# Streaming a weight block's columns in shorter runs: five half groups of an embedding interaction kernel

## The chip, the cores and the metric

The kernel runs on one core of a Trainium2 chip. The core has a matrix engine (TensorE, PE in the profile, whose weight loads have a row of their own, PEld), a vector engine (DVE), a scalar engine (ACT), a general engine (GpSimd, POOL) and a queue engine that starts transfers (SyncE, SP). Two memories on the core matter here: SBUF, which holds the operands, and PSUM, into which PE writes and adds up its results. The metric is the device time of one execution in microseconds; lower is better.

## The reference

For a batch `x` of 1024 rows with 512 features, and a weight tensor `W` of 64 embeddings by 512 features by 512 outputs, the reference computes

```
out_lin     = x @ lin_w.T + lin_b                              # 1024 x 512
xv          = einsum('bf,efm->bem', x, weight)                 # 1024 x 64 x 512
zp          = einsum('bf,efm->bem', x**2, weight**2)
interaction = 0.5 * sum over e of (xv**2 - zp)                 # 1024 x 512
out         = out_lin + interaction
```

Nearly all of the work is `xv`: for each of the 512 outputs ("features" in the title of the change: columns of the result), 64 embeddings of a 512 long dot product, for 1024 rows. It is squared and summed over the 64 embeddings. The sum over `e` doesn't depend on the order of the embeddings, and the order in which the columns are worked through changes no value, as long as each product lands at its own place.

## The kernel before

**Layout.** Before the launch, W is laid out so that one block of it, 128 partitions by 2 by 512, holds in each row of 512 the columns of 8 outputs (`MI = 8`) with 64 embeddings each (`E = 64`): column number = 64 * output + embedding. So the 64 embeddings of one output lie next to each other, 256 bytes of float32. Two such half blocks per group and 16 groups (`NG`) make 32 half groups (`NH`), numbered `h` from 0 to 31.

**Products.** In each half group the matrix product is cut by a Strassen-like scheme into seven block products, numbered 1 to 7 and worked in the order of `ORDER = (1, 6, 2, 3, 7, 5, 4)`; product 5 in that row is the one of the next half group. The seven sums of the blocks of x (`X1` to `X7`) are made once at the start, and the sums of the blocks of W for each half group by transfers that add and by DVE.

**Three pieces.** PE takes each operand in a reduced float32 form, so W's block is split by ACT, POOL and DVE into a high, a low and a combined piece (`pH`, `pL`, `pK`, made in `split`), and so is x (`X1H`, `X1L`, `X1K` and so on). A product is the sum of three: H by H and L by L (`front`), and later K by K (`back`), with a step of DVE or ACT that scales the bank in between. `mm` (L708 to L714) issues them. Each matmul keeps 128 by 128 of x as the stationary operand (the `lhsT`) and streams 512 columns of a piece of W past it, writing them into one PSUM bank (`buf[bank, j]`, 128 by 512 float32). In a half group these are 7 products by 2 halves by 2 banks by 3 pieces by 2 parts of the contraction = 168 matmuls.

**After a product.** DVE or ACT takes the banks: products 1 and 5 are kept in SBUF (`p1`, `p5`), others are added to those, and for products 2, 3, 7 and 4 `finish` squares the finished bank with ACT (L369, `sq<-bank`) and DVE sums the squares over the embeddings (L394, `acc<-sq`). These read the banks in storage order.

**Order.** The whole program is first collected in a `Plan`, which is given a cost for each operation (`PASS`, 0.2267 us for a matmul of this kind) and a fixed order for PE (`key`), and works out one fixed order of instructions for each engine. PE's matmuls of one product's `back` stand some steps after its `front` (`LAG`), between those of the next product.

**Ends.** At the start PE does the linear part in full float32 (L520, L531); at the end it does the product of the squares, `zp`, from sums already taken over the embeddings (L870).

Of the kernel before, what the change touches and what calls it, by code (L numbers as in the profile page):

```python
# [18 lines left out]
P = 128  # L19
# [16 lines left out]
PIECES = {"H": 3, "L": 3, "K": 3}  # L36
SQ, WSQ = 2, 1
PAIRS = {"p1": 2, "w": 2, "p5": 3}

NONE = ""  # L40

# [224 lines left out]
def kernel(  # L266
# [31 lines left out]
    MI = MG // 4  # L298
# [15 lines left out]
    buf = {}  # L314
# [14 lines left out]
    def ring(tag, n, shape, dtype=F32, pool=sb):  # L329
        return ring_of([make(f"{tag}_{i}", shape, dtype, pool) for i in range(n)])  # L330
# [7 lines left out]
    square, wsquare = ring("sq", SQ, block), ring("wsq", WSQ, block)  # L338
    kept = {n: ring(n, size, block) for n, size in PAIRS.items()}
    pairs = [f"{n}_{i}" for n, size in PAIRS.items() for i in range(size)]  # L340
    for n in pairs:
# [7 lines left out]
    def both_of(n):  # L349
        return (n, 0), (n, 1)  # L350
# [16 lines left out]
    def act(o, i, func, reads, writes, size=1024, scale=1.0, bias=0.0):  # L367
        def emit(_):
            nc.scalar.activation(o, i, func, bias=bias, scale=scale)  # L369

        plan.add({ACT: 0.06 + 0.89 * size / 1024}, emit, reads, writes)

    def stt(o, i, scalar, j, op, reads, writes, size=512, both=False):
        def emit(_):
            return nc.vector.scalar_tensor_tensor(o, i, scalar, j, ALU.mult, op)  # L375

        plan.add({DVE: 0.06 + 1.08 * size / 1024}, emit, reads, writes, both=both)

    def dve(o, a, b, sub, reads, writes, size=512, both=False):
        def emit(_):  # L380
            return (nc.vector.tensor_sub if sub else nc.vector.tensor_add)(o, a, b)  # L381

        plan.add({DVE: 0.06 + 1.08 * size / 1024}, emit, reads, writes, both=both)
# [73 lines left out]
    def a_parts(*names):  # L457
        return tuple((n, k) for n in names if n in quads for k in range(KH)) + tuple(
            n for n in names if n not in quads)
# [50 lines left out]
    def four():  # L510
        return [both_of(banks()) for _ in range(4)]
# [142 lines left out]
    def prepare(h, p):  # L654
        if p == 5:
            if h:
                load(h, "T", 0)
                load_more(h, "T", 1)
                load(h, "w11", 0)
                load(h, "w12", 1)  # L660
            else:
                sum_of("T", "w11", "w12")
            w_squares(h, "w12")
        if p == 1:
            if h:
                load(h, "w22", 3)
            else:
                for q in (0, 1, 3, 2):
                    load(h, QUAD[q], q)
            w_squares(h, "w11")  # L670
        if p == 6:
            if h:
                load_more(h, "T", 3)
                load(h, "w21", 2)
            else:
                sum_of("T", "T", "w22")
            w_squares(h, "w22")
        if p == 2:
            w_squares(h, "w21")
        if p == 7:  # L680
            load_more(h, "w12", 3)
        if p == 4:
            load_more(h, "T", 2)
        n = now[h, RHS[p]]
        return n if not h and p in PLAIN else split(n, SPLIT[p] if h else FIRST[p])
# [5 lines left out]
    def finish(h, p, half, bank):  # L691

        row, col = {2: (0, 0), 3: (0, 1), 4: (1, 0), 7: (1, 1)}[p]
        sq, a, names = square(), acc_name[h // NCB], both_of(bank)
        m, b = (2 * col + h % NCB) * MI, row * NJ + 2 * half
        if p == 7:
            n, p5 = value["w", h, half], value["p5", h, half]
            dve(buf[n], buf[bank], buf[p5], True, (p5, *names), (n, *names), 1024)
        act(buf[sq], buf[bank], AF.Square, names, (sq,), scale=S)
        reduce(buf[a][:, b:b + 2, m:m + MI], buf[sq], (sq,), ((a, b // 2, m),))  # L700

    def product(h, p):
        ops, plain = prepare(h, p), not h and p in PLAIN
        for half in range(2):
            bank = banks()
            o, names = buf[bank], both_of(bank)

            def mm(x, w, j, first, bank=bank, half=half):  # L708
                for k in range(KH):
                    made = nc.tensor.matmul(  # L710
                        buf[bank, j], buf[x][:, k, ts(2 * half + j, P)], buf[w][:, k, :],
                        start=first and k == 0, stop=k == KH - 1, skip_group_check=True,
                    )
                return made  # L714

            addend = {6: "p1", 2: "p1", 3: "w", 7: "w", 4: "w"}.get(p)
            addend = addend and value[addend, h, half]
            given = addend and (addend, *names)
            for j in range(2):
                at = slot[0]  # L720
                slot[0] += 1
                if plain:
                    x = OPERAND[p]
                    plan.add({PE: 2 * WHOLE}, lambda _, mm=mm, j=j: mm(x, ops, j, True),
                             (*a_parts(x), ops), ((bank, j),), key=at)
                    continue

                def front(_, mm=mm, j=j):
                    mm(f"X{p}H", ops[0], j, True)
                    return mm(f"X{p}L", ops[1], j, False)  # L730

                def back(_, mm=mm, j=j):
                    return mm(f"X{p}K", ops[2], j, False)

                plan.add({PE: 4 * PASS}, front, (f"X{p}H", f"X{p}L", *ops[:2]), ((bank, j),),
                         key=at)
                late.append((back, (f"X{p}K", ops[2], (bank, j)), (bank, j), slot[0] - j))
            if plain:
                if addend:
                    stt(o, o, U, buf[addend], ALU.add, given, names, 1024)  # L740
            else:
                if addend:
                    stt(o, o, 1 + U, buf[addend], ALU.add, given, names, 1024)
                elif SCALE[p] == ACT:
                    act(o, o, AF.Copy, names, names, scale=1 + U)
                else:
                    plan.add({DVE: 1.14}, lambda _, o=o: nc.vector.tensor_scalar(
                        o, o, 1 + U, None, ALU.mult), names, names)
                for back, reads, write, at in late:
                    plan.add({PE: 2 * PASS}, back, reads, (write,), key=at + LAG + 0.5 + 0.1 * write[1])  # L750
                late.clear()
            if p in (1, 5):
                n = value[f"p{p}", h, half] = kept[f"p{p}"]()
                act(buf[n], o, AF.Copy, names, (n,), scale=U if plain else 1.0)
            if p == 6:
                n, p5 = kept["w"](), value["p5", h, half]
                value["w", h, half] = n
                dve(buf[n], o, buf[p5], False, (p5, *names), (n,), 1024)
            if p in (2, 3, 7, 4):
                finish(h, p, half, bank)  # L760
# [24 lines left out]
    for h in range(NH):  # L785
        for p in ORDER:
            if p != 5:
                product(h, p)
            elif h + 1 < NH:
                product(h + 1, p)  # L790
            if not h and p == 1:
                product(h, 5)
            if not h:
                give_back(*(n for n in ("A11", "A12", "A22") if OPERAND[p] == n))
        if h % NCB == NCB - 1 and h + 1 < NH:
            turn(h // NCB)
# [5 lines left out]
    for r, pieces in enumerate((("X5H", "X5L", "X5K"), ("X1H", "X1L", "X1K"))):  # L802
# [7 lines left out]
        else:  # L810
            half = (("w2h", r),)
# [30 lines left out]
    for (r, c), n in zip(BLOCKS, ("p1", "p1", "p5", "p5")):  # L842
        n = o_name[r, c] = kept[n]()
# [41 lines left out]
    b = four()  # L885
    key = slot[0]
    for at, (r, c) in enumerate(BLOCKS):
        n = o_name[r, c]
# [63 lines left out]
```

## Time and profile before

| | |
|---|---|
| time, median of 2 runs | 1282.32 us (1282.12 and 1282.51) |
| profiled execution, first to last instruction (span) | 1280.3 us; its time with what lies around the span is not listed apart |
| PE, matmuls | 1274.3 us busy, 5524 instructions |
| PEld, weight loads | 1033.4 us busy, 5524 instructions |
| DVE | 1233.0 us busy |
| POOL | 1053.9 us busy |
| ACT | 967.0 us busy |
| granted PE clock | 1.000 |

How to read it: busy time is the time in which an engine has at least one instruction under way. [...] A full float32 matmul shows as two rows in the profile, so 38 of them make the profile's 5524 rows out of 5486 matmuls of the program.

### The profile page before, as it was taken

Reading aid. Unit: us, or ns where it says so; the run is one execution under the profiler, and the core shown is the slowest. Engines: PE = TensorE matmul, PEld = TensorE weight load, DVE = VectorE, ACT = ScalarE, POOL = GpSimd, SP = SyncE. Lnnn points to the kernel's source line nnn. Section 1 sums busy time; section 2 is a strip of 40 time slices with the busy share of each in tenths; the row PEclk is TensorE's granted clock in tenths of the full one; section 3 lists DMA queues with packets and bytes.
Section 4 is the critical chain, followed back from the end, with each engine's and each line's share of the span. In section 5 each row is a group of like instructions: output and inputs, shape, how many; then the busy total and the mean of one; then the engine's idle time right before and its main releaser. Section 6 shows DMA issues by size and latency. Waiting matters only on the chain.

```text
span 1280.3 us, 15588 instructions
## 1 busy us (share of the span) xinstructions
PE 1274.3 (100%) x5524; PEld 1033.4 (81%) x5524; DVE 1233.0 (96%) x1014; ACT 967.0 (76%) x1008; POOL 1053.9 (82%) x533
## 2 busy tenths in 40 slices
PE   9999999999999999999999999999999999999998
PEld 4788888888888888888888888888888888888886
DVE  6999999999999999999999999999999999999997
ACT  7677787777787777877677877777788777788891
POOL 2988898888898888898888898888888888889884
PEclk9999999999999999999999999999999999999999
DMA  7766654446664555755455664555665444664647
GB/s 229 176 173 146 148 129 109 105 119 140 148 142 109 95 122 133 153 130 135 92 115 130 148 153 102 115 115 117 152 146 130 102 106 119 148 152 117 138 99 184
DMA packets 67646, 170.36 MB, mean 133 GB/s; under 512 B 22896, under 2 KB 23920, under 8 KB 67568
## 3 DMA queue, kind: packets, MB, share of 16 engines
q0 software_dynamic: 20160, 71.84, 30.7%
q1 hardware_dynamic: 45584, 95.18, 25.6%
q10 hardware_dynamic: 1824, 2.36, 0.5%
q8 instruction: 43, 0.70, 0.2%
q14 instruction: 35, 0.29, 0.1%
HBM read 158.86 MB, written 6.29 MB: 129 GB/s over the span
## 4 chain that ended last, share of the span: by engine, by line
PE 97%; DVE 2%; ACT 1%; issue 0%; DVEq 0%; ACTq 0%
PE bank L710 93%; PE bank L870 2%; PE bank L531 1%; DVE bank L375 1%; PE bank L520 1%; DVE acc L394 1%; PE bank L548 0%; DVE w L381 0%; ACT sq L369 0%; DVE w_sum L394 0%; DVE X1K L375 0%; DVE p L375 0%; DVE X1L L375 0%; ACT pL L369 0%; ACT pH L369 0%
## 5 line engine op out<-in xcount | busy, mean ns | idle before, releaser
L387 POOL TENSOR_TENSOR pK<-pH,pL 128x1024 fp32r<-128x1024 f32 x224 | 591.1, 2639 | 180.2 <-PE bank L710 169.5
L369 ACT ACTIVATE sq<-bank 128x1024 f32<-128x1024 f32 x256 | 261.9, 1023 | 93.2 <-issue 46.8
L394 DVE TENSOR_REDUCE acc<-sq 128x16 f32<-128x1024 f32 x256 | 308.0, 1204 | 0.2 <-ACT sq L369 0.2
L387 POOL TENSOR_TENSOR pL<-T,pL 128x1024 fp32r<-128x1024 f32 x95 | 238.1, 2506 | 1.0 <-ACT pL L369 1.0
L375 DVE SCALAR_TENSOR_TENSOR bank<-bank,w 128x1024 f32<-128x1024 f32 x192 | 234.2, 1220 | 0.4
L381 DVE TENSOR_TENSOR w<-bank,p 128x1024 f32<-128x1024 f32 x128 | 155.6, 1216 | 25.1 <-PE bank L710 25.1
L387 POOL TENSOR_TENSOR pL<-w,pL 128x1024 fp32r<-128x1024 f32 x65 | 175.4, 2699 | 0.0
L369 ACT ACTIVATE p<-bank 128x1024 f32<-128x1024 f32 x128 | 131.0, 1023 | 56.0 <-PE bank L710 56.0
L375 DVE SCALAR_TENSOR_TENSOR pL<-pH,w 128x1024 fp32r<-128x1024 f32 x62 | 168.1, 2712 | 0.0
L369 ACT ACTIVATE pL<-T 128x1024 fp32r<-128x1024 f32 x95 | 100.0, 1053 | 73.4 <-issue 71.0
L394 DVE TENSOR_REDUCE w_sum<-wsq 128x16 f32<-128x1024 f32 x128 | 154.3, 1205 | 0.0
L375 DVE SCALAR_TENSOR_TENSOR bank<-bank,p 128x1024 f32<-128x1024 f32 x128 | 152.9, 1216 | 0.0
L369 ACT ACTIVATE pH<-w 128x1024 fp32r<-128x1024 f32 x128 | 135.2, 1056 | 11.6 <-PE bank L710 11.3
L369 ACT ACTIVATE wsq<-w 128x1024 f32<-128x1024 f32 x128 | 135.0, 1054 | 4.0 <-DVE w_sum L394 4.0
L369 ACT ACTIVATE pL<-w 128x1024 fp32r<-128x1024 f32 x66 | 70.0, 1061 | 43.4 <-PE bank L710 25.0
L369 ACT ACTIVATE pH<-T 128x1024 fp32r<-128x1024 f32 x96 | 101.2, 1054 | 0.0
L406 POOL DMA_DIRECT2D T<-weight x94 | 83.3, 981 | 9.1 <-POOL pL L387 9.0
L710 PE MATMUL bank<-pH,X4H 128*128 128x512 f32 x256 | 81.4, 399 | 0.1
L710 PE MATMUL bank<-pH,X5H 128*128 128x512 f32 x256 | 79.2, 391 | 0.0
L710 PE MATMUL bank<-pL,X4L 128*128 128x512 f32 x256 | 79.2, 390 | 0.0
L710 PE MATMUL bank<-pL,X5L 128*128 128x512 f32 x256 | 78.8, 389 | 0.0
L710 PE MATMUL bank<-pH,X6H 128*128 128x512 f32 x256 | 78.8, 389 | 0.0
(142 smaller groups left out, 2586.5 us busy)
## 6 DMA issues: line engine op xcount, KB each, us to landing
w<-weight SPq DMA_DIRECT2D x128, 512.0 KB, 7.5
T<-weight POOLq DMA_DIRECT2D x94, 512.0 KB, 7.4
w<-weight POOLq DMA_DIRECT2D x32, 512.0 KB, 10.2
T<-weight SPq DMA_DIRECT2D x31, 512.0 KB, 6.2
accd<-turned SPq DMA_DIRECT2D x64, 32.0 KB, 8.5
p<-lind SPq DMA_DIRECT2D x4, 512.0 KB, 3.6
w<-xT SPq DMA_DIRECT2D x6, 256.0 KB, 5.3
lind<-p SPq DMA_DIRECT2D x3, 512.0 KB, 3.6
```

Source lines behind the costliest of these rows:

```text
L369: nc.scalar.activation(o, i, func, bias=bias, scale=scale)
L375: return nc.vector.scalar_tensor_tensor(o, i, scalar, j, ALU.mult, op)
L381: return (nc.vector.tensor_sub if sub else nc.vector.tensor_add)(o, a, b)
L387: return (nc.gpsimd.tensor_sub if sub else nc.gpsimd.tensor_add)(o, a, b)
L394: lambda _: nc.vector.tensor_reduce(o, i.rearrange("p a (m e) -> p a m e", e=E), axis=AX.X, op=ALU.add),
L406: {POOL: 0.62}, lambda _: nc.gpsimd.dma_start(o, i, accum_op=ALU.add),
L520: return nc.tensor.matmul(buf[bank[u]], b[:, k, ts(u, P)], a[:, k, :], start=first and k == 0, stop=k == KH - 1, skip_group_check=True,)
L531: made = nc.tensor.matmul(buf[bank[u]], b[:, k, ts(u, P)], a[:, k, :], start=first and k == 0, stop=k == KH - 1, skip_group_check=True,)
L710: made = nc.tensor.matmul(buf[bank, j], buf[x][:, k, ts(2 * half + j, P)], buf[w][:, k, :], start=first and k == 0, stop=k == KH - 1, skip ...
L870: made = nc.tensor.matmul(buf[bank[u]], w[:, k, (2 * c + u) * P:(2 * c + u + 1) * P], x[:, k, :], start=z == 0 and i == which[0] and k == ...
```

## The change

A table `ORDERS` names five half groups and a number of parts for each: half group 4 with 2 parts, 7 with 4, 10 with 8, 13 with 16 and 16 with 32. In these, `in_order` gives the matmul another view of the same 512 columns, for the moving operand and for the PSUM bank alike: the 64 embeddings of each output are cut into that many parts, and the columns are streamed part by part, in each part output by output, in each output the part's embeddings. With 2 parts a run of neighbouring columns is 32 long (128 bytes), with 32 parts it is 2 long (8 bytes), and from run to run the address jumps by 256 bytes, or back to the next part. Each column still lands at its own place. The stationary operand, the pieces and what reads the banks afterwards stay as they are.

```diff
+ORDERS = {
+    4: 2, 7: 4, 10: 8, 13: 16, 16: 32,
+}
...
+            def in_order(a):
+                n = ORDERS.get(h)
+                return a if n is None else a.rearrange("p (m a b) -> p a m b", m=MI, a=n)
+
             def mm(x, w, j, first, bank=bank, half=half):
                 for k in range(KH):
                     made = nc.tensor.matmul(
-                        buf[bank, j], buf[x][:, k, ts(2 * half + j, P)], buf[w][:, k, :],
+                        in_order(buf[bank, j]), buf[x][:, k, ts(2 * half + j, P)],
+                        in_order(buf[w][:, k, :]),
                         start=first and k == 0, stop=k == KH - 1, skip_group_check=True,
                     )
```

On PE, at the place where half group 16 begins (its product 5, between the matmuls of half group 15's products 3, 7 and 4), the program has these rows before the change. A row names the line, the bank, the piece of W and the piece of x, the shape written, and how many equal ones follow each other.

```order
L710 MATMUL bank_117<-pK_101,X3K 128x512 x4
L710 MATMUL bank_116<-pH_97,X5H 128x512 x2
L710 MATMUL bank_116<-pL_100,X5L 128x512 x2
L710 MATMUL bank_116<-pH_97,X5H 128x512 x2
L710 MATMUL bank_116<-pL_100,X5L 128x512 x2
L710 MATMUL bank_114<-pK_102,X7K 128x512 x4
L710 MATMUL bank_117<-pH_97,X5H 128x512 x2
```

At the same place the changed program has these:

```order
L717 MATMUL bank_117<-pK_101,X3K 128x512 x4
L717 MATMUL bank_116<-pH_97,X5H 128x32x8x2 x2
L717 MATMUL bank_116<-pL_100,X5L 128x32x8x2 x2
L717 MATMUL bank_116<-pH_97,X5H 128x32x8x2 x2
L717 MATMUL bank_116<-pL_100,X5L 128x32x8x2 x2
L717 MATMUL bank_114<-pK_102,X7K 128x512 x4
L717 MATMUL bank_117<-pH_97,X5H 128x32x8x2 x2
```

Nothing has moved: the shape written has become 32 parts by 8 outputs by 2 embeddings in the rows of half group 16, and the line number is 717 for 710. On PE again, where half group 4 begins, the changed program has the rows below; before the change all of them read 128x512.

```order
L717 MATMUL bank_116<-pH_97,X5H 128x2x8x32 x2
L717 MATMUL bank_116<-pL_100,X5L 128x2x8x32 x2
L717 MATMUL bank_114<-pK_102,X7K 128x512 x4
L717 MATMUL bank_117<-pH_97,X5H 128x2x8x32 x2
L717 MATMUL bank_117<-pL_100,X5L 128x2x8x32 x2
L717 MATMUL bank_115<-pK_102,X7K 128x512 x4
```

Over the whole program the shape is another in 5 by 168 = 840 matmuls. No row stands at another place on PE, and on DVE, ACT, POOL and SP the rows are the same apart from the line numbers.

## The prediction, made before the changed kernel ran

> **What bounds the kernel now.** I read the shares of busy time first, then PE's waits, then the chain that ends last, and then PE's rows one by one. On the page of the kernel before:
>
> ```profile
> PE 1274.3 (100%) x5524; PEld 1033.4 (81%) x5524; DVE 1233.0 (96%) x1014; ACT 967.0 (76%) x1008; POOL 1053.9 (82%) x533
> ...
> PEclk9999999999999999999999999999999999999999
> ...
> PE 97%; DVE 2%; ACT 1%; issue 0%; DVEq 0%; ACTq 0%
> PE bank L710 93%; PE bank L870 2%; PE bank L531 1%; DVE bank L375 1%; PE bank L520 1%; DVE acc L394 1%; PE bank L548 0%; DVE w L381 0%; ACT sq L369 0%; DVE w_sum L394 0%; DVE X1K L375 0%; DVE p L375 0%; DVE X1L L375 0%; ACT pL L369 0%; ACT pH L369 0%
> ```
>
> PE is busy for the whole span and makes up 97% of the chain that ended last, 93% of it on the one line that the change edits. A busy PE alone says little, because its rows overlap. What counts is whether it ever waits. The view of PE's waits has two rows:
>
> ```profile
> PE bank L870 <- ACT sq L369: 1.0, 1, 1.0
> PE bank L548 <- PEq L941: 0.8, 1, 0.8
> ```
>
> Two waits in 1280 us, 1.8 us together, and both outside the main loop. DVE at 96% is close behind, but it never holds PE up. So the time is the number of matmuls by the distance from one to the next, and there is nowhere for a slower matmul to hide. The view of the waits of all engines shows that the others stand behind PE:
>
> ```profile
> POOL pK L387 <- PE bank L710: 169.5, 91, 3.0
> ACT p L369 <- PE bank L710: 56.0, 48, 1.7
> DVE w L381 <- PE bank L710: 25.1, 59, 0.6
> ```
>
> PE's distance is read from its rows in order of time (start, length of the merged row, what):
>
> ```profile
> 200.52 1.07 PE L710 MATMUL bank<-pK,X6K 128*128 128x512 f32 x4
> 201.43 0.62 PE L710 MATMUL bank<-pH,X2H 128*128 128x512 f32 x2
> ...
> 202.78 0.62 PE L710 MATMUL bank<-pL,X2L 128*128 128x512 f32 x2
> 203.24 1.07 PE L710 MATMUL bank<-pK,X6K 128*128 128x512 f32 x4
> ```
>
> From 200.52 to 203.24 us are 12 matmuls (4, then 8), 2.72 us, so **0.2267 us a matmul**, or 0.443 ns for each of its 512 columns. A half group of 168 takes 168 x 0.2267 = 38.1 us, and the five that change 190.4 us.
>
> **The change part by part.**
>
> *Nothing is removed, added or moved.* The five half groups have the same 840 matmuls, weight loads, banks, transfers and waits at the same places, so the term of the instruction count is zero, and no wait is added behind which anything could queue. Only the addresses differ that PE walks through in reading W's piece and in writing the bank. A pass could not get shorter by that: it streams the same 512 columns, and PE has no wait to lose but those 1.8 us. The lower bound is therefore nothing.
>
> *What a jump in the addresses costs PE* no row of this trace shows: every matmul of the loop reads and writes 128x512 in one run. I bound it from above by rows of slower walks over the same tiles. The first is PE's own, in the linear part, full float32, two rows to a matmul:
>
> ```profile
> 22.80 7.03 PE L531 MATMUL bank<-w,p 128*128 128x512 f32 x16
> 29.67 4.88 PE L710 MATMUL bank<-w,w 128*128 128x512 f32 x11
> ```
>
> 16 rows in 29.67 - 22.80 = 6.87 us are 0.4294 us for 512 columns, 0.203 us over 0.2267: PE at about half pace. The second is ACT, which reads two banks, 1024 columns, in 1.023 us:
>
> ```profile
> L369 ACT ACTIVATE sq<-bank 128x1024 f32<-128x1024 f32 x256 | 261.9, 1023 | 93.2 <-issue 46.8
> ```
>
> That is 1.0 ns a column, so 512 columns in 0.512 us, 0.285 over a matmul. By these, 840 matmuls would cost 840 x 0.203 = 170 us at PE's half pace and 840 x 0.285 = 239 us at ACT's, and nothing at full pace. The bounds are far apart, so the form of the cost decides. The five half groups cut the run by two each time: 32, 16, 8, 4 and 2 columns. If memory hands out values in portions, a run costs nothing while it fills whole portions and the pace halves at the first run that fills half of one. Where that step lies the trace doesn't say. The nearest supported price for a step is PE's own half pace, and the likeliest place is the shortest run, since it is hit in every case in which any is.
>
> **The sum I take:** half groups 4, 7, 10 and 13 at nothing, half group 16 at half pace. The price of half pace lies between 0.4294 - 0.2267 = 0.203 us (PE's float32 row) and 0.2267 us (a matmul twice as long): 168 x 0.203 = 34 us to 168 x 0.2267 = 38 us. I take 36. Against the profiled execution that is 1280.3 + 36 = 1316.3 us of span. What lies around the span is 2.0 us by the median of the runs (1282.3 - 1280.3), so 1282.3 + 36 = **1318 us**, 2.8% more.
>
> *Does anything cover it?* Two rows could. The weight load of the next matmul runs beside the current one:
>
> ```profile
> L710 PEld LDWEIGHTS bank<-pL,X4L 128*128 128x128 f32 x256 | 48.1, 188 | 10.5
> ```
>
> 188 ns of load in a matmul's 227 leave 39 ns idle, so the load would not hold back a longer matmul. Half of the float32 row is 0.2147 us, 12 ns under 0.2267; if those 12 ns are not streaming but something beside it, jumps that cost up to 12 ns a matmul are hidden. At half pace this takes at most 168 x 0.012 = 2 us off, inside the range. What the other engines do about a slower PE is also covered. The stretch with most of half group 16 (its matmuls begin with the 2671st of 5486; 120 of the 147 here are its own, by the count) is, before:
>
> ```profile
> 640.00:673.00 33.00, 33.00 (x147) 27.11 (x146) 32.61 (x27) 25.23 (x28) 27.00 (x15) 1.00 0.53 118
> ```
>
> The columns after the first are PE, PEld, DVE, ACT and POOL. DVE is busy 32.6 of 33 us; with PE at half pace all of them wait for banks and then start again with full buffers, so nothing is late afterwards. It also means that the loss isn't won back: after it PE again runs at 0.2267 us and not faster.
>
> [...]
>
> **The rivals.**
>
> 1. *No change:* pairs of columns are enough for full pace, and jumps cost nothing or vanish in the 12 ns. For it: the row of 0.4294 us shows that the walk and the arithmetic need not be the same limit, and the shortest run is still a pair. Against it: 256 jumps in each matmul of half group 16, through two memories, with 0.443 ns for each column. Time: 1282 us, up to 1286. It decides if the address walk fetches no more than two columns at a time. This is the case that ends on the other side, not slower.
> 2. *A price for every jump,* whatever the run. The five half groups have 16, 32, 64, 128 and 256 runs in a matmul, 496 together. At one column's time, 0.443 ns, that is 168 x 496 x 0.443 = 37 us, less up to 9 us by the 12 ns of cover; at ACT's 1.0 ns it is 83 us. Time: 1310 to 1365 us. For it: no portions need to be assumed. The total is near my forecast at its low end, but the rows would tell: half group 13 then pays half of what 16 pays, while I say nothing.
> 3. *The step comes one or two cuts earlier.* Half group 13 slow as well: 2 x 36 = 72 us if both go at half pace, 1354 us; if 13 goes at half and 16 at quarter pace (3 x 0.2267 more), 36 + 114 = 150 us, 1432 us.
> [...]
>
> That the change doesn't do what it says is excluded: the program has the new shapes in all 840 matmuls.
>
> **How the numbers follow.** My forecast, only half group 16 at half pace: 0.36. No change: 0.26. A price per jump: 0.14. An earlier step: 0.12, of it 0.07 near 1354 us. All at half pace: 0.10. Something else, a small gain included: 0.02. The likeliest gives 1318 us. The range goes from 1281 us, just under no change, to 1400 us; it holds the forecast, no change, the price per jump and the nearer half of the earlier step, 0.36 + 0.26 + 0.14 + 0.07 = 0.83, and leaves out the far steps. A measurement of this kernel can tell about 2%, 25.6 us, from no change. Faster than that needs a gain for which I found no place: 0.02. Within it lie no change and a per-jump price that is mostly covered: 0.28. Slower: 0.70.
>
> **What the profile of the changed kernel would show.** PE still has no waits in the loop, the clock stays at full, and PE's busy count stays at 5524. With rows kept apart by shape, or read in order of time, matmuls of half groups 4, 7, 10 and 13 stand 0.227 us apart, and those of half group 16 0.43 to 0.45 us; the stretch that held 147 matmuls in 33 us takes some 60 us; DVE's share in it falls to about half, and POOL's wait for PE's banks grows by some 10 to 20 us. **What would make me wrong:** a distance above 0.24 us already in half groups 4, 7 or 10 (rivals 2 to 4), a cost that doubles from one to the next (rival 2), 0.227 us in half group 16 (rival 1), or a new wait of PE in the loop, which would mean that reading SBUF in another order holds up another engine first.

## The result, and the profile after

The changed kernel takes **1344.38 us** (two runs, 1344.32 and 1344.43) against 1282.32 us: 1.0483 times as long, 95% interval 1.0466 to 1.0500, or 62 us more. The span of its profiled execution is 1342.6 us, 62.3 us longer.

The first lines of its page answer to those shown of before:

```profile
PE 1336.5 (100%) x5524; PEld 1039.9 (77%) x5524; DVE 1240.3 (92%) x1014; ACT 971.9 (72%) x1008; POOL 1054.0 (79%) x533
...
DVE  6999999999999899989854899999999999999997
...
PEclk9999999999999999999999999999999999999999
...
PE 97%; DVE 2%; ACT 1%; issue 0%; DVEq 0%; ACTq 0%
```

PE is busy for 62 us more with the same 5524 instructions, at the same clock; POOL's busy time stays, DVE's and ACT's grow by 7 and 5 us, far less than PE's. DVE's row in 40 slices has a dent near the middle (half group 16) and a few smaller ones before. PE's own waits are still two, at the same places:

```profile
PE bank L878 <- ACT sq L372: 1.0, 1, 1.0
PE bank L551 <- PEq L949: 0.8, 1, 0.8
```

So nothing new holds PE up; its matmuls are slower. Where, a view of five stretches of 32 us shows, each inside the time that the changed kernel spends on one changed half group (columns: stretch, its length, then busy time and number of instructions of PE, PEld, DVE, ACT and POOL, then clock and transfers). PE works matmuls of the half groups before and after it in between, up to 24 of a stretch's 138. Before the change the same stretches of time read alike, whichever half group they hold:

```profile
189.00:221.00 32.00, 32.00 (x143) 26.44 (x142) 31.00 (x26) 23.64 (x26) 25.99 (x14) 1.00 0.46 97
...
680.00:712.00 32.00, 32.00 (x143) 26.33 (x142) 32.00 (x26) 23.10 (x25) 26.09 (x15) 1.00 0.50 113
```

After:

```profile
189.00:221.00 32.00, 32.00 (x138) 25.53 (x137) 30.54 (x25) 22.43 (x25) 25.21 (x13) 1.00 0.46 87
305.00:337.00 32.00, 32.00 (x136) 25.45 (x135) 30.76 (x25) 21.13 (x22) 25.01 (x13) 1.00 0.42 85
422.00:454.00 32.00, 32.00 (x128) 24.17 (x127) 29.68 (x23) 21.07 (x22) 22.82 (x12) 1.00 0.44 89
543.00:575.00 32.00, 32.00 (x118) 22.43 (x117) 28.38 (x22) 19.00 (x19) 20.91 (x11) 1.00 0.35 68
680.00:712.00 32.00, 32.00 (x67) 13.56 (x66) 16.71 (x13) 9.46 (x10) 12.79 (x6) 1.00 0.06 9
```

PE is busy throughout, but gets through 142 or 143 matmuls in each stretch before, and 138, 136, 128, 118 and 67 after (a count takes in two or three that reach over the stretch's ends). Read exactly, from the start of one PE row to the start of the next in the trace, averaged over the places where both belong to the same half group (157 of its 168). The rows overlap (before the change a row of the loop lasts 390 ns on average, with 227 ns to the next one's start), so it is the distance that adds up to the time:

```
half group                  4      7      10     13     16    the other 26 from 1 to 31
run, columns                32     16     8      4      2     512
distance before, ns        227.3  227.3  227.3  227.3  227.3  227.2
distance after, ns         236.3  238.9  255.6  277.7  491.6  227.5
```

Over all 168 matmuls of each the means are 236.3, 238.7, 255.0, 277.8 and 491.3 ns. Against the same matmuls before the change that is 9.0, 11.5, 27.8, 50.5 and 264.0 ns more, times 168: 1.5, 1.9, 4.7, 8.5 and 44.4 us, together 61.0 of the 62 us. Most of the rest, 1.1 us, lies in half groups 5, 8, 11, 14 and 17, right behind the changed ones. (The expectations below count from 227.6 ns, the mean before the change over all matmuls of this kind, which takes in slower ones at the program's start.)

### The profile page after: what moved, and what is told of

Its sections match the earlier page's. It is cut to its first block, busy times and chain, and to the rows that moved or that the text cites. A ratio compares the mean times of both kernels' runs of the same rounds, so it can differ in the third digit from the quotient of the medians.

```text
span 1342.6 us, 15588 instructions
## 1 busy us (share of the span) xinstructions
PE 1336.5 (100%) x5524; PEld 1039.9 (77%) x5524; DVE 1240.3 (92%) x1014; ACT 971.9 (72%) x1008; POOL 1054.0 (79%) x533
## 4 chain that ended last, share of the span: by engine, by line
PE 97%; DVE 2%; ACT 1%; issue 0%; DVEq 0%; ACTq 0%
PE bank L717 93%; PE bank L878 2%; PE bank L534 1%; DVE bank L378 1%; PE bank L523 1%; DVE acc L397 1%; PE bank L551 0%; DVE w L384 0%; ACT sq L372 0%; DVE w_sum L397 0%; DVE X1K L378 0%; DVE p L378 0%; DVE X1L L378 0%; ACT pL L372 0%; ACT pH L372 0%
## 5 line engine op out<-in xcount | busy, mean ns | idle before, releaser
L378 DVE SCALAR_TENSOR_TENSOR bank<-bank,w 128x1024 f32<-128x1024 f32 x192 | 234.2, 1220 | 11.5 <-PE bank L717 11.1
L390 POOL TENSOR_TENSOR pL<-w,pL 128x1024 fp32r<-128x1024 f32 x65 | 172.5, 2653 | 0.0
L378 DVE SCALAR_TENSOR_TENSOR pL<-pH,w 128x1024 fp32r<-128x1024 f32 x62 | 171.8, 2770 | 0.0
L717 PE MATMUL bank<-pH,X5H 128*128 128x512 f32 x256 | 82.6, 404 | 0.0
L717 PE MATMUL bank<-pL,X4L 128*128 128x512 f32 x256 | 82.3, 403 | 0.0
L717 PE MATMUL bank<-pH,X6H 128*128 128x512 f32 x256 | 82.0, 402 | 0.0
L717 PE MATMUL bank<-pL,X5L 128*128 128x512 f32 x256 | 82.0, 402 | 0.0
```

Of the source, the lines that this page charges most:

```text
L390: return (nc.gpsimd.tensor_sub if sub else nc.gpsimd.tensor_add)(o, a, b)
L717: made = nc.tensor.matmul(in_order(buf[bank, j]), buf[x][:, k, ts(2 * half + j, P)], in_order(buf[w][:, k, :]), start=first and k == 0, st ...
```

## The experiments

Each experiment is read by the same distances. Where an edit isn't shown in full, only the table `ORDERS` and the call of `in_order` differ from the changed kernel.

**Which side pays, the read or the write?** Two kernels with the new order on one side only.

```diff
-                        in_order(buf[bank, j]), buf[x][:, k, ts(2 * half + j, P)],
+                        buf[bank, j], buf[x][:, k, ts(2 * half + j, P)],
                         in_order(buf[w][:, k, :]),
```

> PE reads W's pieces in the new order of runs in the five half groups, but writes the bank's columns in one run, so the products land in other columns of the bank; the work is the same. In the changed kernel the distances from matmul to matmul are 236, 239, 255, 278 and 491 ns in half groups 4, 7, 10, 13 and 16 (227.6 elsewhere). Theory R, the price is that of reading SBUF in short runs: the same five distances and 1344 us. Theory W, the price is that of writing PSUM in short runs: 227 ns in all five and 1282 us. Theory B, the two sides hold each other up, each for a part: distances between, and the excesses of the two one-sided kernels add up to that of the changed one.

```diff
                         in_order(buf[bank, j]), buf[x][:, k, ts(2 * half + j, P)],
-                        in_order(buf[w][:, k, :]),
+                        buf[w][:, k, :],
```

> PE reads W's pieces in one run, but writes the bank in the new order of runs in the five half groups, so the products land in other columns; the work is the same. Theory R (reading SBUF sets the price): 227 ns in all five half groups and 1282 us. Theory W (writing PSUM sets it): 236, 239, 255, 278 and 491 ns and 1344 us. Theory B (a part each): between, the excesses adding up to those of the changed kernel.

Reading in the new order alone: 1343.75 us. Writing alone: 1282.07 us, with the kernel before at 1282.10 us on the same chip. The stretches of the kernel that only reads so:

```profile
189.00:221.00 32.00, 32.00 (x138) 25.53 (x137) 30.54 (x25) 22.44 (x24) 25.23 (x12) 1.00 0.46 94
...
680.00:712.00 32.00, 32.00 (x67) 13.72 (x66) 16.07 (x12) 8.82 (x10) 12.15 (x6) 1.00 0.08 13
```

and of the one that only writes so, each again inside its half group:

```profile
189.00:221.00 32.00, 32.00 (x143) 26.44 (x142) 31.00 (x26) 23.62 (x26) 26.02 (x14) 1.00 0.49 97
...
646.00:678.00 32.00, 32.00 (x143) 26.50 (x142) 31.36 (x26) 24.14 (x26) 26.10 (x14) 1.00 0.52 104
```

The distances are 236.3, 238.9, 254.2, 277.7 and 491.6 ns with the read alone and 227.3 ns in all five with the write alone. Theory R holds in all five half groups: the whole price is that of reading SBUF in short runs, and the bank takes 256 runs of two columns as fast as one run of 512. That is shown for the orders written here, runs of 2 to 32 columns with jumps of 256 bytes.

**Is that so for other jumps too?** Pairs again on the write side alone, with five other jumps.

```diff
-    4: 2, 7: 4, 10: 8, 13: 16, 16: 32,
+    4: 2, 7: 4, 10: 8, 13: 16, 16: 64,
...
-                return a if n is None else a.rearrange("p (m a b) -> p a m b", m=MI, a=n)
+                return a if n is None else a.rearrange("p (m a b) -> p a m b", a=n, b=2)
```

> W's pieces are read in one run; the bank is written in pairs, with jumps of 16, 32, 64, 128 and 512 bytes in half groups 4, 7, 10, 13 and 16, so the products land in other columns. Pairs with jumps of 256 bytes cost nothing on the write side. Theory R, a pair is enough for the bank whatever the jump: 227 ns in all five, 1282 us. Theory D, it depends on the jump, and 256 bytes was a lucky one: one or more of the five above 240 ns, 1285 us or more.

1281.88 us (before, on the same chip: 1282.98), and 227.2 or 227.3 ns in all five. Theory R. The write side is settled for pairs with jumps of 16 to 512 bytes. Single columns on the write side were not tried.

**What does the read pay for, jumps or portions?** The same five jumps, pairs on both sides:

> All five half groups read and write runs of 2 columns, 256 runs a matmul; only the jump from run to run differs: 16, 32, 64, 128 bytes in half groups 4, 7, 10 and 13, and 512 bytes in 16 (256 bytes cost 264 ns a matmul in the changed kernel). Theory P, memory hands out portions of which a pair fills only a part, and every jump to another portion costs the same: about 490 ns in all five, 5 x 168 x 0.264 = 222 us more, 1504 us. Theory D, the price depends on the jump's length, since what lies far apart falls on the same part of the memory: short jumps cheaper, the distance rising from about 250 ns at 16 bytes to 490 or more at 512 bytes, 1340 to 1450 us.

1469.26 us: 451.9, 460.0, 430.2, 450.3 and 446.3 ns for jumps of 16, 32, 64, 128 and 512 bytes. One stretch inside each half group:

```profile
198.00:230.00 32.00, 32.00 (x74) 14.91 (x73) 16.75 (x13) 9.62 (x11) 12.41 (x6) 1.00 0.01 2
350.00:382.00 32.00, 32.00 (x74) 15.05 (x73) 16.95 (x13) 9.17 (x9) 11.27 (x5) 1.00 0.04 7
504.00:536.00 32.00, 32.00 (x77) 15.54 (x76) 17.30 (x14) 11.19 (x12) 12.69 (x6) 1.00 0.12 23
655.00:687.00 32.00, 32.00 (x74) 15.03 (x73) 17.07 (x13) 9.96 (x10) 12.72 (x6) 1.00 0.02 2
810.00:842.00 32.00, 32.00 (x74) 15.07 (x73) 18.53 (x15) 10.46 (x11) 12.69 (x6) 1.00 0.12 21
```

A jump over two columns already halves the pace (451.9 ns), and the farther ones cost about as much (430 to 460 ns). That is P in the main: the five lie within 7% of each other, at 1.9 to 2.0 times 227.3 ns. The 491 ns at 256 bytes in the changed kernel, which P took as the common price, is the outlier.

Then runs that begin off a 16-byte boundary, on the read side alone:

```diff
-    4: 2, 7: 4, 10: 8, 13: 16, 16: 32,
+    4: (1, 2), 7: (16, 2), 10: (8, 2), 13: (16, 1), 16: (64, 0),
...
+                n, shift = ORDERS[h]
+                at = k * (N - 4) + shift
+                flat = a.rearrange("p k n -> p (k n)")[:, at:at + N]
+                return flat.rearrange("p (m a b) -> p a m b", m=MI, a=n)
```

> Only the read is changed (the bank is written in one run), and in four of the five half groups it begins 1 or 2 columns off a boundary of 16 bytes, so other columns of W's piece are multiplied; the work is the same. Half group 4: one run of 512, 2 off. 7: runs of 4, 2 off. 10: runs of 8, 2 off. 13: runs of 4, 1 off. 16: single columns, not off. Theory P, W's piece is fetched in portions of 16 bytes (4 columns) that begin at multiples of 16 bytes, one portion each 1.7 to 1.9 ns (487 ns for the 256 pairs, 227 for the 128 portions of one run): 129, 256, 192, 256 and 512 portions give 227, 430 to 490, 330 to 360, 430 to 490 and 860 to 970 ns, about 1490 us. Theory J, each jump has a price, wherever the run begins: 227, 278, 255, 278 as without the offset, and for the 512 single columns some 750 ns (491 and 264 more), 1395 us.

1434.20 us. Its stretches:

```profile
189.00:221.00 32.00, 32.00 (x138) 25.87 (x137) 30.68 (x26) 22.74 (x24) 25.32 (x13) 1.00 0.44 88
313.00:345.00 32.00, 32.00 (x72) 14.56 (x71) 15.10 (x11) 9.32 (x10) 8.74 (x5) 1.00 0.08 15
467.00:499.00 32.00, 32.00 (x95) 18.46 (x94) 22.83 (x17) 13.55 (x15) 14.26 (x8) 1.00 0.29 54
623.00:655.00 32.00, 32.00 (x71) 14.38 (x69) 15.74 (x13) 11.99 (x12) 15.82 (x8) 1.00 0.21 47
762.00:794.00 32.00, 32.00 (x70) 14.45 (x69) 16.16 (x13) 9.65 (x10) 8.15 (x4) 1.00 0.14 28
```

One run, 2 columns off: 235 ns. Runs of 4: 485 ns when 2 off and 459 when 1 off, where the same runs on the boundary took 278. Runs of 8, 2 off: 352 ns, for 255 on the boundary. The jumps are the same in both; only the boundary differs, so theory J falls, and the portion is 16 bytes: as long as a run uses all four columns of each portion the pace stays near full (226 to 278 ns in the runs of 4), and where it uses fewer it is near half. The runs of 8 fit: 2 off, half of their columns lie in whole portions and half in parts of one, which by an estimate from 227 and 485 ns makes 356, and 352 were measured. But P failed at its last point. Single columns, 512 portions, took 494 ns and not 860 to 970: as much as pairs. So the pace doesn't go down with the number of portions; in these orders it has two levels, and columns of a portion that a run uses only in part are read at the lower one. Two columns of a portion were not enough (430 to 491 ns in the pairs so far), four were.

**Do the parts add up?** The new order in half group 16 alone, and in the other four alone.

```diff
-    4: 2, 7: 4, 10: 8, 13: 16, 16: 32,
+    16: 32,
```

> The changed kernel with the new order in half group 16 alone (runs of 2). By the distances of the changed kernel it carries 168 x (491.3 - 227.6) = 44.3 us of the 62. If PE's distances simply add up: 1282.3 + 44.3 = 1326.6 us, ratio 1.0345. My prediction had 36 us for it, 1318 us. If the other half groups' slower matmuls shift a wait into the loop, the parts don't add up to 62 us.

```diff
-    4: 2, 7: 4, 10: 8, 13: 16, 16: 32,
+    4: 2, 7: 4, 10: 8, 13: 16,
```

> The changed kernel with the new order in half groups 4, 7, 10 and 13 alone. By the distances: 168 x (8.7 + 11.1 + 27.4 + 50.2) ns = 16.4 us, 1298.7 us, ratio 1.0128, and the two parts add up to the 62 us. My prediction had nothing for them, 1282 us.

1326.97 us, 1.0345 times before (1.0329 to 1.0360), and 1299.44 us, 1.0132 times (1.0115 to 1.0149), against 1282.35 us. That is 44.6 and 17.1 us, together 61.7 of the 62. The distances are those of the changed kernel (491.6; 236.3, 238.9, 255.2, 277.7). The prices add up as on a chain with one engine.

**What are the small prices of whole portions?** Runs of 32, 16, 8 and 4 columns use whole portions and still cost 9 to 50 ns a matmul. Is it a price for runs, or a fixed one?

```diff
-                return a if n is None else a.rearrange("p (m a b) -> p a m b", m=MI, a=n)
+                return a if n is None else a.rearrange("p (m a b) -> p a m b", m=n, a=2)
```

> Each half group's 512 columns are taken as 2, 4, 8, 16 or 32 stretches (half groups 4, 7, 10, 13, 16) cut in two parts each: 4, 8, 16, 32 or 64 runs a matmul of 128, 64, 32, 16 or 8 columns. Theory F, a pattern in more than one run has a fixed price of some 7 ns a matmul and about 0.35 ns a run beside it: 236, 237, 236, 240 and 255 ns, (8 + 9 + 9 + 12 + 28) x 0.168 = 11 us more, 1293 us. Theory J, only jumps have a price, 0.4 to 0.55 ns each: 229, 231, 236, 242 and 255 ns, 9 us more, 1291 us. The two part at 4 and 8 runs: 8 to 9 ns or 2 to 4 ns.

1286.25 us (before: 1282.10), and 227.4, 227.4, 236.2, 240.3 and 232.5 ns for 4, 8, 16, 32 and 64 runs. Both theories fall. A pattern in several runs has no fixed price, and 64 runs of 8 with jumps of 64 bytes cost less (232.5) than 16 runs of 32 with 256 (236.2) or 64 runs of 8 with 256 (255.6). The jump's length matters. So, with runs of 4 and five other jumps (the table has parts 2, 4, 8, 32 and 64, the view `a=n, b=4`):

> All five half groups read and write runs of 4 columns that fill one portion of 16 bytes; the jump is 32, 64, 128, 512 and 1024 bytes in half groups 4, 7, 10, 13 and 16 (256 bytes: 278 ns in the changed kernel). Theory P alone, whole portions are read at full pace and the 50 ns belong to the run's length: 270 to 285 ns in all five, 5 x 168 x 0.05 = 42 us more, 1324 us. Theory B, portions that follow each other at certain distances fall on the same part of SBUF, or on the one that the weight load reads: distances of 227 to 300 ns that differ by the jump, short jumps (32 and 64 bytes) below 250 ns, 1290 to 1320 us.

1298.70 us: 232.7, 227.1, 245.9, 267.7 and 250.6 ns for 32, 64, 128, 512 and 1024 bytes. As theory B had it, the price goes by the jump, and with 64 bytes it is gone. Half of B is about the weight load, which reads SBUF beside the stream (its rows, 188 ns each before the change, lie beside PE's). To test that half, the load's addresses were changed:

```diff
-                        in_order(buf[bank, j]), buf[x][:, k, ts(2 * half + j, P)],
+                        in_order(buf[bank, j]), buf[x][:, k, (2 * half + j) * P:(2 * half + j) * P + 1].to_broadcast([P, P]),
```

> The changed kernel, but in all matmuls of the loop the stationary operand's 128 columns are all the block's first one, so that the weight load reads one address in each partition; the products are therefore others, the count of instructions is the same. [...] Theory L, the smaller prices are collisions of the moving read with the next weight load's read: 227 ns in half groups 4, 7, 10 and 13, some 440 ns in 16, 1318 us. Theory N, the load has no part in it: 236, 239, 255, 278 and 491 ns, 1344 us.

1358.61 us, longer than the changed kernel: 233.5, 238.7, 232.3, 276.8 and 490.8 ns, and 231.7 ns in the other half groups, where it was 227.5. Neither theory. With the load's addresses the distance changes too (from 227.5 to 231.7 ns where W is read in one run), so the stationary operand has a part in it, but the prices in half groups 7, 13 and 16 stay to within 1 ns: there they don't hang on which columns the load reads. That the load as such has no part in them is not shown, since it still reads SBUF for every matmul. The load's rows are longer beside the slow read: in half group 16 they take 187.7 ns on average before the change and with the write alone, 206.0 ns in the changed kernel and 205.9 ns with the read alone. The 232.3 ns of half group 10 prove nothing about the load, as the next experiment shows.

**All orders in one kernel.** Half groups 1 to 31 have an order each.

> Half groups 1 to 31 each stream in an order of their own, reading and writing alike: runs of 4, 8, 16, 32, 64 and 128 columns with every jump from 32 to 1024 bytes that fits (21 orders in half groups 1 to 21), then seven of them again (22 to 27, 30, 31) with other buffers, and pairs with jumps of 1024 and 64 bytes in 28 and 29. Theory B (portions that are read too close after each other from the same part of SBUF, by the stream itself or by the next weight load, hold the read up): the distance depends on the jump more than on the number of runs, the same order gives the same mean within 4 ns when it comes again, runs of 64 and 128 columns 227 ns, some orders under 227.6 ns, none under 213; pairs 430 to 490. Theory J (a price for each jump): the distance falls with the run's length whatever the jump, 4 columns the dearest at 270 ns, and no order under 227 ns. The whole: B 1380 to 1420 us, J 1450 us.

1389.14 us. The mean distances in ns, by run and jump (several numbers: the order came in several half groups):

```
jump, bytes      32            64                    128          256      512      1024
run 4            232.7 233.2   225.1 226.9 226.0     246.2        277.7    267.5    251.1 250.4
run 8                          232.7 232.5 232.4     230.1 225.0  242.4    231.8    243.1
run 16                                               239.7        238.9 239.9  232.3  239.9
run 32                                                            236.4    233.8    236.3
run 64                                                                     227.5    227.2
run 128                                                                             227.3
run 2 (pairs)                  460.6                                                339.2
```

Theory B in the main, J not at all: down a column or along a row the price doesn't follow the number of runs. An order that came again gave the same mean within 5.1 ns, 1 ns over the limit set. But runs of 8 with jumps of 256 bytes took 242.4 ns in half group 9 and 255.6 in half group 10 of the changed kernel, and pairs with 64 bytes 460.6 in one half group and 430.2 in another. The single distances show what the means hide. In the middle of a half group they settle into a short round that comes again and again, whatever the product and the piece, and the same order can settle into different rounds:

```
run  jump, bytes  half group, kernel         distances that come round, ns
8    256          10, changed kernel         246 267 254 263 277 247
8    256          9, this kernel             233 233 234
8    128          8, this kernel             229 230 230 237 228
8    128          24, this kernel            219 221
2    64           10, pairs, five jumps      430 to 433
2    64           29, this kernel            473 473 474
```

So the order alone doesn't set the price; the round that a half group falls into does too. Half group 10 of the kernel whose load reads one column, 225 and 222 ns in turn, may be no more than another round. What decides on the round (the place of the buffers, or what was under way before) is not shown, and that portions fall on the same part of SBUF, the reason that theory B gives, is not shown either. Pairs with jumps of 1024 bytes at 339 ns don't fit a pair's fixed price either: in that order each portion is read again after one other. That it is still at hand then would explain it, but was only argued.

**A faster order?** One order lay under the 227.3 ns of a single run each time it came in the table: runs of 4 with jumps of 64 bytes. It was given to half groups 1 to 31.

```diff
+ORDERS = {h: (4, 4) for h in range(1, 32)}
...
+                n, b = ORDERS[h]
+                return a.rearrange("p (m a b) -> p a m b", a=n, b=b)
```

> Runs of 4 columns with jumps of 64 bytes in half groups 1 to 31, reading and writing: the one order whose mean distance was under that of one run (226.0 ns over 471 matmuls, 218 to 240, against 227.3). If the distance is set by the addresses alone, 31 x 168 = 5208 matmuls save 1.3 ns each, 6.8 us, ratio 0.995. If it depends on neighbours that are streamed in one run, or on chance, 227 ns or more and no gain: ratio 1.000 or above.

1278.54 us against 1282.59 us, ratio 0.9969 (0.9957 to 0.9981): 4 us faster than before, with 226.5 ns over 5201 matmuls (227.2 before). Its page's line of busy times:

```profile
PE 1270.3 (99%) x5524; PEld 1031.9 (81%) x5524; DVE 1231.1 (96%) x1014; ACT 965.9 (76%) x1008; POOL 1049.7 (82%) x533
```

PE is busy for 4.0 us less than before (1274.3). It is the expected mechanism at a smaller size (4 for 6.8 us), since the mean came out at 226.5 and not 226.0 ns, and it beats both kernels.

## Why the prediction was right, and where it was wrong

**What bounds the kernel: right.** PE has the same two waits as before and the time grew by the sum of its distances, 61.0 of 62 us from the five half groups alone. Nothing hid a slower matmul and nothing won it back; the 44.6 and 17.1 us of the two parts measured alone add up to the whole.

**The direction and the range: right; the size too small.** 62 us came for 36. The step that failed is the sum: "half groups 4, 7, 10 and 13 at nothing, half group 16 at half pace", and both of its terms were too small. That the range held 1344 us is owed in part to its width, which was there for the rivals: by the working of the forecast alone, half pace in half group 16 gave 34 to 38 us.

- *Half group 16.* The mechanism, a step at a run shorter than a portion, was right: the shifted runs show the portion, 16 bytes (runs of 4 at 278 ns on its boundary, at 485 and 459 ns off it). Its price was 264.0 ns a matmul and not 203 to 227, 44 us for 36. The bound from PE's float32 row (429 ns) and from a doubled matmul (453) holds for pairs with jumps of 16, 128 and 512 bytes (446 to 452 ns), not with 32 (460) and 256 (491), the one in the change, and with 64 in one half group of two (430 and 461).
- *Half groups 4, 7, 10 and 13.* I put them at nothing, on the premise that "a run costs nothing while it fills whole portions". They cost 17.1 us. Whole portions are not free when the jump is of a bad length: runs of 4 went from 226 to 278 ns with the jump alone.

**The cover of 12 ns: not seen, and not decided.** Half group 4 has 16 runs a matmul, 15 jumps at 0.443 ns or 6.6 ns by the price I gave rival 2, and should have been hidden. It paid 9.0 ns. A dearer jump that is hidden in part would look the same, and about 7 of the 227 ns are in fact not the streaming of 512 columns, since half group 24 of the kernel with all orders went at 220 ns for 47 matmuls in a row.

**The rivals.** No change was right for the write side and only there. A price for every jump gave 1310 to 1365 us, and the time lies in it, but for the wrong reason: 64 runs cost 232.5 or 255.6 ns by the jump's length, and moving 128 runs of 4 off the boundary raised 278 to 485. The earlier step (1354 us) would need half pace in half group 13, which had 278 ns. All at half pace, to which I gave 0.10, no run of these five orders shows: half groups 4, 7, 10 and 13 went at 236 to 278 ns in the changed kernel and with the read alone, and all five at 227.3 ns with the write alone.

**What the profile was to show.** DVE's share in half group 16 fell to half (16.7 of 32 us), as said. The 147 matmuls that took 33 us take 64 and not some 60. POOL's wait for the banks grew by 38 us and not 10 to 20:

```profile
POOL pK L390 <- PE bank L717: 207.8, 98, 9.4
```

The distance "above 0.24 us already in half groups 4, 7 or 10", named as what would make me wrong, came in half group 10 (255 ns).

**What stays open:** what sets the price of a jump. The runs show that it lies on the read side (236.3 to 491.6 ns with the read alone, 227.3 ns with the write alone), that it depends on the jump's length (226 to 278 ns in runs of 4), that one order can settle at more than one price (runs of 8 with jumps of 128 bytes at 220 and 231 ns), and that the weight load's addresses have a part at least where W is read in one run (227.5 and 231.7 ns). Whether parts of SBUF collide, and which, the runs don't tell.

## What to carry to other kernels

Where PE is busy throughout, the order in which a 4-byte moving operand is read is a cost like any other: keep runs on 16-byte boundaries and at least four columns long, since below that these matmuls went at about half pace (430 to 494 ns for 227, and 339 in one order). If an order must be permuted, permute it on the PSUM side, where runs of two columns cost nothing at six jump lengths (227.2 or 227.3 ns), and measure the jump on the read side, since with whole portions it decided between 226 and 278 ns. One profile can price many variants: 31 half groups with an order each gave 23 prices in one run. Give each variant more than one half group, and read the single distances beside the mean: the same order came out at 225 and at 230 ns.

## What was unexpected in the hardware

- Single columns are read as fast as pairs: 494 and 491 ns for 512 columns, both with jumps of 256 bytes. The price doesn't follow the number of columns that a run uses of a portion.
- One run isn't the fastest order. In half group 24 of the kernel with all orders, runs of 8 with jumps of 128 bytes, 47 matmuls in a row stood 220 ns apart (219 and 221 in turn), where one run gives 226 or 227 nearly always. If all 5208 matmuls of half groups 1 to 31 stayed in that round, some 37 us would be saved, by an estimate from 227.2 and 220.0 ns, and not the 4 us found here. Nothing here shows how to keep them in it: in half group 8 the same order settled at 231 ns on average.
- The distances repeat from one kernel to another, but not always by place. Between the changed kernel and the one that only reads in its order, the same matmul of half group 13 differs by 0.3 ns and of half group 16 by 0.6 ns on average, while within half group 16 they range from 486 to 535 ns. In half group 10 it differs by 9.8 ns, although the means are within 1.4 ns: the round of six distances is the same in both kernels, three matmuls apart.
